# Layer 0 attention: four uneven chains of additions in place of four equal ones, row sums taken at other key tiles, five plus two buffers made four plus three

## The chip, the cores and the metric

The kernel runs on one NeuronCore of a Trainium2 chip. TensorE (PE) multiplies matrices into PSUM, ScalarE (ACT) here takes exponentials and copies PSUM out, VectorE (DVE) adds, normalizes and transposes, GpSimd (POOL) does a few powers and memsets, and SyncE issues most of the DMAs. Every engine works through its own instructions in order and waits on semaphores for the others. The metric is the device time of one execution in microseconds (us), the median of several runs. Lower is better.

## The reference

The program is a network of four layers on a tensor of 2 x 128 x 64 x 64 float32 values. The change lies in the first of the two attentions of layer 0, cut here to what matters:

```python
q1, k1, v, q2, k2 = map(to_heads, (q1, k1, v, q2, k2))      # 2 batches, 4 heads of 32 channels, 4096 tokens
q1, q2, k1, k2 = map(l2norm_tokens, (q1, q2, k1, k2))
attn1 = softmax(einsum('bhnc,bhmc->bhnm', q1, k1) * temperature, axis=-1)
out1 = einsum('bhnm,bhmc->bhnc', attn1, v)
attn2 = softmax(einsum('bhnc,bhnd->bhcd', q2, k2) * temperature, axis=-1)
out2 = einsum('bhnc,bhcd->bhnd', v, attn2)
out = out1 + out2                                            # then w_po, a norm, w_proj and the residual
```

For each query the softmax needs the sum of 4096 exponentials. Scores are bounded (the queries and keys have norm one), so the kernel takes the exponentials without a maximum, adds them up beside the product with the values, and divides at the end.

## The kernel before

**Tiling.** `attention` (from L1824) runs once for each of the two batches. The queries are cut into 8 blocks of 512 (`qb`), the keys into 32 tiles of 128 (`kt`). Its loop has 8 x 32 = 256 steps, counted by `n`; keys lie on the partitions, so a step makes a tile of weights of 128 keys x (4 heads x 512 queries), 1 MB.

**One step** has this order in the program:

1. `scores(n)` (L1850): eight matmuls into four PSUM banks. Head 0 goes to bank 6 (`single`), which every step uses again; heads 1 to 3 go to three banks (`three`) that alternate between banks 0 to 2 and 3 to 5.
2. At some steps, `totals` (L1842, operand `ones`): the row sums. Four matmuls with a matrix of ones for each of two chains of added weights, into the third bank of the other half (`banks[:, other + 2, :]`), which the step before used for scores.
3. The exponential of `single` (L1918, 512 columns) and that of `three` (L1923, 1536 columns) on ScalarE, into the tile `held[n]`, called `weights`.
4. After a `totals`, `emptied` (L1889): ScalarE copies the row sums to the tile `total`, of which there is one buffer.
5. `multiply(n - 2)` (L1842, operand `vt`): four matmuls of the weights made two steps ago with the values, gathered over the 32 key tiles in bank 7. After the last key tile ScalarE copies bank 7 to the columns of `q1` (L1863). At `kt` 1 this `multiply`, the one with the copy, stands between the two exponentials.
6. `add(n)` (L1873): VectorE adds the weights to a running sum.
7. Some steps after a `totals`, `normalized` (L1895 to L1904): VectorE turns the row sums; for the first half of a block it keeps them, for the second it adds both, takes the reciprocal, turns it back and scales the columns of `q1`.

**The chains.** `add` keeps two chains side by side, one for even and one for odd key tiles. `SUMMED = 16` restarts both every 16 key tiles, so a block of queries has four chains of 8 tiles. The first tile of a chain is not added: the chain starts as that tile of weights itself, and the second tile is added to it into a tile `sums`. No addition is thus made at `kt` 0, 1, 16 and 17, and 28 additions are made in a block. A finished chain goes to `pending`; two finished chains make a `totals`, at `kt` 18 and at `kt` 2 of the next block (`kt % SUMMED == 2`). `normalized` follows at `kt` 22 and 6.

**Side work.** At every fourth step (`n % 4 == 3`) the generator `side` is advanced: the channel attention (L1775 on), and, in the first batch, the normalization of the second batch's input, or, in the second, the statistics of the first batch's output. It puts transposes on PE, copies on ScalarE and statistics on VectorE between the steps of query blocks 0 to 5 of the first batch, and 0 to 2 of the second.

**Order.** `_in_order` ties all instructions of an engine to the order in which the program writes them, so none of them overtakes another. The pool `f0_p` holds five buffers of `weights` and two of `sums`, 1 MB each, and small tiles. A buffer is used again when all who read it are done.

Of the kernel before, what the change touches and what calls it, by code (L numbers as in the profile page):

```python
# [10 lines left out]
F32 = mybir.dt.float32  # L11
# [7 lines left out]
CH = 512  # L19
NCH = S // CH  # L20
ROWS = CH // W
NQT = S // 128
# [1262 lines left out]


LIMIT = 60.0
SUMMED = 16
F32R = mybir.dt.float32r
I32 = mybir.dt.int32  # L1290

# [157 lines left out]
def _layer0(ctx, tc, X, a, cst, worst, there, dram):  # L1449
# [8 lines left out]
    def sp():  # L1458
        n = at["pair"]
        at["pair"] = (n + 1) % 3  # L1460
        return banks[:, 2 * n : 2 * n + 2, :]

    def acc(n):
        return banks[:, 6 + n, :]

    def half():
        if at["spare"] is None:
            return sp()[:, 0, :]
        return banks[:, at["spare"].pop(0), :]
# [361 lines left out]
    def attention(pool, side):  # L1831

        sums = acc(1)
        single = banks[:, 6, :]
        parts, pending, totalled, by_query = [None, None], [], [], {}
        last = NCH * NQT - 1
        held = {}

        def four(out, lhs, w, first, stop):
            for j in range(4):  # L1840
                rows = slice(32 * j, 32 * j + 32)
                nc.tensor.matmul(out[rows, :], lhs(rows), w[:, j, :], start=first, stop=stop)  # L1842

        def scores(n, three):
            qb, kt = n // NQT, n % NQT
            for j in range(4):
                rows = slice(32 * j, 32 * j + 32)
                bank = single if j == 0 else three[:, j - 1, :]
                for h in range(2):
                    nc.tensor.matmul(  # L1850
                        bank[64 * h : 64 * h + 64, :],
                        k1[rows, kt * 128 + 64 * h : kt * 128 + 64 * h + 64],
                        q1[rows, qb * CH : (qb + 1) * CH],
                        start=True,
                        stop=True,
                    )

        def multiply(n):
            qb, kt = n // NQT, n % NQT
            w = held.pop(n)  # L1860
            four(sums, lambda rows: vt[:, kt, rows], w, kt == 0, kt == NQT - 1)
            if kt == NQT - 1:
                nc.scalar.copy(q1[:, qb * CH : (qb + 1) * CH], sums)  # L1863

        def add(n):
            p, i, w = n % 2, n % SUMMED // 2, held[n]
            if i == 0:
                parts[p] = w
            else:
                t = parts[p]  # L1870
                if i == 1:
                    parts[p] = pool.tile([128, 4, CH], F32, tag="sums", name="sums", bufs=2)
                nc.vector.tensor_add(  # L1873
                    parts[p].rearrange("p j c -> p (j c)"),
                    t.rearrange("p j c -> p (j c)"),
                    w.rearrange("p j c -> p (j c)"),
                )
            if i == SUMMED // 2 - 1:
                pending.append((n // NQT, n % NQT < SUMMED, parts[p]))

        def totals(bank):
            (qb, first, a), (_, _, b) = pending.pop(0), pending.pop(0)
            four(bank, lambda rows: ones, a, True, False)
            four(bank, lambda rows: ones, b, False, True)
            return qb, first, bank

        def emptied(qb, first, bank):
            t = pool.tile([128, CH], F32, tag="total", name="total", bufs=1)
            nc.scalar.copy(t, bank)  # L1889
            totalled.append((qb, first, t))  # L1890

        def normalized(qb, first, t):
            cols = slice(qb * CH, (qb + 1) * CH)
            turned = pool.tile([128, CH // 32, 32], F32, tag="turned", name="turned", bufs=1)
            nc.vector.transpose(turned.rearrange("p n i -> p (n i)"), t)  # L1895
            if first:
                by_query[qb] = small.tile([128, CH // 32], F32, tag="first", name="first")
                nc.vector.tensor_copy(by_query[qb], turned[:, :, 0])
                return
            rec = small.tile([128, CH // 32], F32, tag="rec", name="rec")  # L1900
            nc.vector.tensor_add(rec, turned[:, :, 0], by_query.pop(qb))
            nc.vector.reciprocal(rec, rec)
            nc.vector.transpose(turned, rec.unsqueeze(2).to_broadcast([128, CH // 32, 32]))
            nc.vector.tensor_mul(  # L1904
                q1[:, cols], q1[:, cols], turned.rearrange("p n i -> p (n i)")
            )

        for n in range(last + 1):
            kt = n % NQT
            mine, other = 3 * (n % 2), 3 * ((n + 1) % 2)  # L1910
            three = banks[:, mine : mine + 3, :]
            at["spare"] = [other, other + 1]
            held[n] = pool.tile([128, 4, CH], F32, tag="weights", name="weights", bufs=5)
            scores(n, three)
            total = None
            if len(pending) == 2 and kt % SUMMED == 2:
                total = totals(banks[:, other + 2, :])
            nc.scalar.activation(held[n][:, 0, :], single, AF.Exp)  # L1918
            if n % 4 == 3:
                next(side, None)  # L1920
            if kt == 1 and n > 1:
                multiply(n - 2)
            nc.scalar.activation(held[n][:, 1:, :], three, AF.Exp)  # L1923
            if total:
                emptied(*total)
            if kt != 1 and n > 1:
                multiply(n - 2)
            add(n)
            if totalled and kt % SUMMED == 6:
                normalized(*totalled.pop())  # L1930
        at["spare"] = None
        multiply(last - 1)
        multiply(last)
        for _ in side:
            pass
        emptied(*totals(half()))
        normalized(*totalled.pop())

# [81 lines left out]
    for b in range(B):  # L2020
        w2 = small.tile([128, 128], F32, tag="w2", name="w2")
        with tc.tile_pool(name="f0_conv", reuse_waits="tile", bufs=1) as pool, _in_order(tc):
            ss2, own = convolutions(pool, b, before)
        if b == 0:

            with _after(tc):
                rows_of_weights = _weights_by_rows(nc, dram, a)
        side = [channel_attention(ss2, own, w2)]
        if b + 1 < B:
            side.append(normalize(b + 1))  # L2030
        if b:
            side.append(
                _stats_steps(
                    nc,
                    small,
                    half,
                    X[:, b - 1, :],
                    cst,
                    mhalf,
                    there[:, b - 1],  # L2040
                    by_scalar=True,
                )
            )
        with tc.tile_pool(name="f0_p", reuse_waits="tile", bufs=4) as pool, _in_order(tc):
            attention(pool, chain(*side))
        before = finish(b, w2)
# [532 lines left out]
```

## Time and profile before

| | |
|---|---|
| median of the runs, with the lowest and the highest | 4082.22 us (4076.9 to 4084.47, 3 runs) |
| the profiled execution: its own time, and its span | 4084.82 us, 4082.9 us |
| mean granted TensorE clock | 0.98 |
| first attention, from its first exponential to its last row sum | 605.75 us (186.56 to 792.31) |
| second attention, the same | 592.07 us (980.67 to 1572.74) |
| a query block without side work | 71.75 us |
| busy share of the span: PE, DVE, ACT | 95%, 78%, 79% |
| one addition (L1873), 128 x 2048 | 2.28 us, and 2.2 us from one start to the next |

The span is the time from the first to the last instruction. In a line of a timeline the columns are the start and the duration in us, the engine, the line of the code, the operation, the tiles it writes and reads with their shapes, how many instructions are merged, and in brackets how long the engine stood idle before it and which instruction's end released it. In a line for a window they are the window, its length, the busy time of each engine with the number of its instructions, the granted clock of PE, and the DMA share and rate. PE's busy time counts matmuls that overlap each other once.

### The profile page before, as it was taken

To read this page: it belongs to the slowest core of one execution; us is meant where nothing else is said; L and a number is where in the kernel's file an instruction comes from. 1 tells how busy PE (TensorE), PEld (TensorE's weight loads), DVE (VectorE), ACT (ScalarE), POOL (GpSimd) and SP (SyncE) were. 2 spreads that over 40 slices of the span, in tenths; PEclk is the share of its full clock that TensorE was granted. 3 is DMA by queue.
4 is the path that set the end of the run, shared out by engine and by line. 5 is a ranking of instruction groups with operands and counts; after the bars stand their busy time and mean duration, and the time that the engine had idled before them with its cause. 6 is when DMAs were issued, how large, how long until landed. Compare 5 with 4: busy or idle time off the path is not lost.

```text
span 4082.9 us, 82128 instructions
## 1 busy us (share of the span) xinstructions
PE 3876.2 (95%) x35214; PEld 1325.1 (32%) x35214; DVE 3195.3 (78%) x3572; ACT 3245.5 (79%) x3955; POOL 71.1 (2%) x145
## 2 busy tenths in 40 slices
PE   7899999989999998997898999999999999999998
PEld 4511221244111113445665232232223223222222
DVE  5699898766899998986776887777777777776666
ACT  4488888735888984334654899999999999999998
POOL 1000000010000001000000000000000000000000
PEclk9999999999999999998899999999999999999999
DMA  1199970000000000003673210121012000110000
GB/s 50 23 193 187 189 95 2 1 2 2 1 2 2 2 2 13 6 1 128 256 278 112 72 35 29 36 61 32 24 32 70 27 27 29 36 54 6 6 6 4
DMA packets 193128, 217.59 MB, mean 53 GB/s; under 512 B 30441, under 2 KB 154345, under 8 KB 188658
## 3 DMA queue, kind: packets, MB, share of 16 engines
q1 hardware_dynamic: 192754, 212.25, 20.4%
q8 instruction: 278, 4.55, 0.5%
q14 instruction: 96, 0.79, 0.1%
HBM read 178.64 MB, written 98.57 MB: 68 GB/s over the span
## 4 chain that ended last, share of the span: by engine, by line
PE 63%; DVE 8%; issue 3%; ACT 1%; SPq 0%; DMA 0%; POOL 0%; DVEq 0%; POOLq 0%; ACTq 0%
PE ps_acc L2294 25%; PE ps_s L2271 18%; PE ps L1842 5%; PE ps L1850 5%; DVE X L662 3%; PE ps_bank L710 2%; PE ps_z L1008 2%; DVE e L950 1%; DVE sums L1873 1%; PE ps_bank L1062 1%; PE ps_bank L681 1%; PE ps_acc L2152 1%; PE ps_acc L2198 1%; PE ps_pe L925 1%; ACT weights L1923 1%
## 5 line engine op out<-in xcount | busy, mean ns | idle before, releaser
L2285 ACT ACTIVATE weights<-ps_s 128x1024 f32<-128x1024 f32 x1920 | 1781.5, 1062 | 76.0 <-PE ps_s L2271 75.9
L2294 PE MATMUL ps_acc<-weights,vt 128*32 128x512 f32 x8192 | 1092.9, 605 | 0.0
L1873 DVE TENSOR_TENSOR sums<-sums,weights 128x2048 f32<-128x2048 f32 x384 | 852.1, 2284 | 0.1
L2271 PE MATMUL ps_s<-q,k 64*128 64x512 f32 x4096 | 830.3, 469 | 4.2 <-DMA k<-stack 3.0
L1923 ACT ACTIVATE weights<-ps 128x1536 f32<-128x1536 f32 x512 | 741.0, 1447 | 8.5 <-PE ps L1850 8.5
L2271 PEld LDWEIGHTS ps_s<-q,k 64*128 64x128 f32 x4096 | 348.3, 184 | 936.4 <-ACT weights L2285 809.0
L1850 PE MATMUL ps<-q,k 32*64 32x512 f32 x8192 | 574.9, 613 | 3.8 <-ACT weights L1918 3.2
L1842 PE MATMUL ps<-weights,vt 128*32 128x512 f32 x4096 | 549.0, 608 | 0.0
L2243 DVE SCALAR_TENSOR_TENSOR exp_z<-exp_z,exp_m 128x1024 f32<-128x1024 f32 x384 | 469.0, 1221 | 9.3
L1918 ACT ACTIVATE weights<-ps 128x512 f32<-128x512 f32 x512 | 306.9, 599 | 88.7 <-PE ps L1850 51.5
L2227 DVE TENSOR_SCALAR exp_i<-ps_s 128x1024 int32<-128x1024 f32 x128 | 156.7, 1225 | 216.8 <-PE ps_s L2271 216.6
L2294 PEld LDWEIGHTS ps_acc<-weights,vt 128*32 128x32 f32 x8192 | 161.9, 108 | 309.4 <-issue 308.6
L1850 PEld LDWEIGHTS ps<-q,k 32*64 32x64 f32 x8192 | 120.2, 130 | 436.2 <-ACT weights L1918 381.9
L1873 DVE TENSOR_TENSOR sums<-weights 128x2048 f32<-128x2048 f32 x64 | 146.6, 2290 | 107.0 <-ACT weights L1923 97.8
L1842 PEld LDWEIGHTS ps<-weights,vt 128*32 128x32 f32 x4096 | 85.0, 108 | 395.2 <-issue 394.2
L662 DVE SCALAR_TENSOR_TENSOR X<-g,w,X 128x2048 f32<-128x2048 f32 x84 | 197.4, 2351 | 2.6
L2247 DVE SCALAR_TENSOR_TENSOR weights<-exp_z,exp_i 128x1024 f32<-128x1024 f32 x128 | 156.8, 1225 | 15.2
L2243 DVE SCALAR_TENSOR_TENSOR exp_z<-exp_m 128x1024 f32<-128x1024 f32 x128 | 155.9, 1218 | 0.0
L1008 PE MATMUL ps_z<-w_ri,e 128*32 128x128 f32 x2048 | 137.4, 409 | 14.6 <-DVE e L950 12.4
L1613 PE MATMUL ps<-pad,diag 32*32 32x512 f32 x4032 | 141.9, 603 | 4.1 <-ACT vt L1624 3.7
L1842 PE MATMUL ps<-sums,ones 128*32 128x512 f32 x512 | 70.0, 637 | 51.0 <-DVE sums L1873 32.1
L1591 PE MATMUL ps<-xn,w_qkv 128*128 128x512 f32 (+1 forms) x200 | 91.2, 605 | 19.3 <-ACT pad L1598 14.1
(304 smaller groups left out, 2995.9 us busy)
## 6 DMA issues: line engine op xcount, KB each, us to landing
w_ri<-w_r SPq DMA_DIRECT2D x16, 2112.0 KB, 8.0
w_ri<-w_i SPq DMA_DIRECT2D x16, 2112.0 KB, 13.6
stack<-qs SPq DMA_DIRECT2D x64, 256.0 KB, 2.1
q<-stack SPq DMA_DIRECT2D x128, 128.0 KB, 2.5
k<-stack SPq DMA_DIRECT2D x128, 128.0 KB, 2.6
stack<-ks SPq DMA_DIRECT2D x32, 256.0 KB, 2.1
w_r<-in_L_conv_kr_w SPq DMA_DIRECT2D x15, 528.0 KB, 12.5
w_r<-in_L_conv_kr_x SPq DMA_DIRECT2D x15, 528.0 KB, 12.4
```

Source lines behind the costliest of these rows:

```text
L662: nc.vector.scalar_tensor_tensor(xi, g[:, i : i + H // 2, j : j + W], w8[:, s : s + 1], xi, ALU.mult, ALU.add)
L1008: nc.tensor.matmul(out.rearrange("p (n f o) -> p n f o", n=2, f=2), e[:, s, 2 * j : 2 * j + 2, :].rearrange("p f x -> p (f x)"), w.rearran ...
L1842: nc.tensor.matmul(out[rows, :], lhs(rows), w[:, j, :], start=first, stop=stop)
L1850: nc.tensor.matmul(bank[64 * h : 64 * h + 64, :], k1[rows, kt * 128 + 64 * h : kt * 128 + 64 * h + 64], q1[rows, qb * CH : (qb + 1) * CH], ...
L1873: nc.vector.tensor_add(parts[p].rearrange("p j c -> p (j c)"), t.rearrange("p j c -> p (j c)"), w.rearrange("p j c -> p (j c)"),)
L1918: nc.scalar.activation(held[n][:, 0, :], single, AF.Exp)
L1923: nc.scalar.activation(held[n][:, 1:, :], three, AF.Exp)
L2243: nc.vector.scalar_tensor_tensor(z, x, n, m, ALU.add, ALU.mult)
L2247: nc.vector.scalar_tensor_tensor(w.rearrange("p j c -> p (j c)"), z, EXP_TERMS[-1], power, ALU.add, ALU.mult)
L2271: nc.tensor.matmul(ps[j // 2][:, j % 2, :], g.k[kt // 4][rows, j // 2, keys], g.q[qb][rows, j // 2, :], start=True, stop=True,)
L2285: nc.scalar.activation(w[0], ps[p], AF.Exp)
L2294: nc.tensor.matmul(g.ac[32 * j : 32 * j + 32, :], g.vt[:, kt, j // 2, i : i + 2, :].rearrange("p a d -> p (a d)"), w[:, i, :], start=(at = ...
```

## The change

`SUMMED = 16` gives way to `STARTS = (0, 1, 14, 27)`: the key tiles at which a chain starts. The even chain restarts at 14, the odd one at 27. A block of queries now has an even chain of 7 tiles (0 to 12), an odd one of 13 (1 to 25), an even one of 9 (14 to 30) and an odd one of 3 (27 to 31). No addition is made at `kt` 0, 1, 14 and 27; 28 additions are made as before.

The two `totals` of a block stand at `kt` 28 (for the chains of 7 and 13) and at `kt` 1 of the next block (for those of 9 and 3). `normalized` runs at `kt` 0 of the next block for the first and at `kt` 1 for the second; after the last block both run at the end. The exception for `kt` 1 is gone: `multiply(n - 2)` always stands behind both exponentials, and at `kt` 1 also behind `emptied`. The pool has four buffers of `weights` (its default) and three of `sums`.

```diff
 LIMIT = 60.0
-SUMMED = 16
+STARTS = (0, 1, 14, 27)
...
         def add(n):
-            p, i, w = n % 2, n % SUMMED // 2, held[n]
-            if i == 0:
+            p, kt, w = n % 2, n % NQT, held[n]
+            if kt in STARTS:
                 parts[p] = w
             else:
                 t = parts[p]
-                if i == 1:
-                    parts[p] = pool.tile([128, 4, CH], F32, tag="sums", name="sums", bufs=2)
+                if kt - 2 in STARTS:
+                    parts[p] = pool.tile([128, 4, CH], F32, tag="sums", name="sums", bufs=3)
...
-            if i == SUMMED // 2 - 1:
-                pending.append((n // NQT, n % NQT < SUMMED, parts[p]))
+            if kt + 2 in STARTS or kt + 2 >= NQT:
+                pending.append((n // NQT, kt + 2 < NQT, parts[p]))
...
-            held[n] = pool.tile([128, 4, CH], F32, tag="weights", name="weights", bufs=5)
+            held[n] = pool.tile([128, 4, CH], F32, tag="weights", name="weights")
             scores(n, three)
             total = None
-            if len(pending) == 2 and kt % SUMMED == 2:
+            if len(pending) == 2 and kt in (STARTS[-1] + 1, 1):
                 total = totals(banks[:, other + 2, :])
             nc.scalar.activation(held[n][:, 0, :], single, AF.Exp)
             if n % 4 == 3:
                 next(side, None)
-            if kt == 1 and n > 1:
-                multiply(n - 2)
             nc.scalar.activation(held[n][:, 1:, :], three, AF.Exp)
             if total:
                 emptied(*total)
-            if kt != 1 and n > 1:
+            if n > 1:
                 multiply(n - 2)
             add(n)
-            if totalled and kt % SUMMED == 6:
+            if totalled and kt < 2:
                 normalized(*totalled.pop())
         at["spare"] = None
         multiply(last - 1)
         multiply(last)
         for _ in side:
             pass
+        normalized(*totalled.pop())
         emptied(*totals(half()))
         normalized(*totalled.pop())
```

## The prediction

> **What bounds the kernel now.** I read the windows by query block first, then the timeline of one block, then the row groups. In the windows (length, then busy PE, PEld, DVE, ACT, POOL) the lines are query blocks 3 and 6 of the first attention, its sum, block 12 (the fifth of the second attention), and the second sum:
>
> ```profile
> 412.95:490.46 77.51, 73.93 (x828) 15.73 (x820) 69.94 (x65) 68.29 (x76) 5.69 (x3) 0.98 1.06 190
> 642.61:714.37 71.76, 69.06 (x804) 13.46 (x808) 64.57 (x35) 63.73 (x68) 0.00 (x0) 1.00 0.01 2
> ...
> sum 605.75, PE 575.93 PEld 119.68 DVE 545.10 ACT 524.55 POOL 16.55; mean PE 71.99 PEld 14.96 DVE 68.14 ACT 65.57 POOL 2.07
> ```
>
> ```profile
> 1279.62:1351.37 71.75, 69.06 (x804) 13.45 (x808) 65.17 (x36) 63.73 (x68) 0.00 (x0) 1.00 0.01 2
> ...
> sum 592.07, PE 564.53 PEld 112.86 DVE 530.57 ACT 510.62 POOL 3.38; mean PE 70.57 PEld 14.11 DVE 66.32 ACT 63.83 POOL 0.42
> ```
>
> PE is idle 605.75 - 575.93 = 29.8 us and 592.07 - 564.53 = 27.5 us. That is the ceiling of any gain by order alone: 57 us. In a clean block PE is idle 2.69 us. The timeline shows where:
>
> ```profile
> 1247.79 2.28 DVE L1873 TENSOR_TENSOR sums<-sums,weights 128x2048 f32<-128x2048 f32 x1
> 1248.01 1.06 PE L1842 MATMUL ps<-sums,ones 128*32 128x512 f32 x8 [0.64 <-ACT weights L1918]
> 1250.12 1.06 PE L1842 MATMUL ps<-sums,ones 128*32 128x512 f32 x8 [1.04 <-DVE sums L1873]
> ...
> 1254.02 1.11 PE L1850 MATMUL ps<-q,k 32*64 32x512 f32 x16
> 1255.06 1.06 PE L1842 MATMUL ps<-weights,vt 128*32 128x512 f32 x8
> 1256.06 1.11 PE L1850 MATMUL ps<-q,k 32*64 32x512 f32 x16
> ...
> 1282.71 0.59 ACT L1863 COPY q<-ps 128x512 f32<-128x512 f32 x1 [0.46 <-PE ps L1842]
> 1283.20 1.46 ACT L1923 ACTIVATE weights<-ps 128x1536 f32<-128x1536 f32 x1
> 1284.71 1.92 PE L1842 MATMUL ps<-sums,ones 128*32 128x512 f32 x16 [1.01 <-ACT weights L1923]
> ```
>
> A step is 1256.06 - 1254.02 = 2.04 us with no gap on PE: PE sets the pace. At `kt` 18 both chains are late: the last addition ends at 1250.07, the second half of the row sums starts at 1250.12 (the first half follows the addition before, whatever engine the bracket names). At `kt` 2 the row sums wait for the wide exponential of `kt` 1, which stood behind the copy to `q1`. Wait by wait:
>
> ```profile
> L1842 PE MATMUL ps<-sums,ones 128*32 128x512 f32 x512 | 70.0, 637 | 51.0 <-DVE sums L1873 32.1
> ```
>
> 51 of the 57 us of idle PE stand before row sums.
>
> Why is VectorE late there? I subtracted the end of each wide exponential from the start of its addition. In block 12 the lag is 0.03 us at `kt` 2, rises 0.16 to 0.17 per step (an addition every 2.20 us against a step of 2.04), jumps from 0.52 at `kt` 6 to 3.22 at `kt` 7 (the long `normalized`, 2.7 us) and is 4.58 at `kt` 15. It is 0.66 at 18, 0.03 at 19, jumps by 0.9 at 23 (the short `normalized`), and is 2.81 at 31. VectorE is slower than PE only while it adds without a break; each step without an addition gives back.
>
> [...]
>
> **The change, part by part.** Nothing is added or removed in number: 28 additions, 16 row-sum matmuls of ones in groups of four, two copies, two `normalized` a block, no DMA. S is the start of a step's scores. From the rows: the wide exponential ends at S + 3.06 (1256.06 to 1259.12), an addition can start at S + 3.09 and ends 2.29 later, at S + 5.38 + lag; row sums of a step start at S + 1.04, their second half 0.87 later.
>
> 1. *Row sums at 28.* The first half uses the chain that ended at 12. The second needs the addition at 25. Additions restart at 15 with lag 0.03 (11 steps of 0.165 to `kt` 13 make 1.85; two steps, 4.08, pass with one addition, 2.20, and give back 1.88), so the lag at 25 is 0.03 + 10 x 0.165 = 1.7. It ends at S25 + 7.1; the second half is due at S25 + 6.12 + 1.91 = S25 + 8.0. Spare 0.9: no wait. This removes 1.9 us (the first half 1247.3 to 1248.01, the second 1248.9 to 1250.12).
> 2. *Row sums at 1.* Only two steps behind the last addition, which now has lag 0.03 + 2 x 0.165 = 0.35 (three additions after the break at 27) and ends at S31 + 5.7; the second half is due at S31 + 6.0. Spare 0.3. The wide exponential of `kt` 0 ends at S31 + 5.1, the first half is due at S31 + 5.1: just met. As the copy to `q1` now stands behind both exponentials, the 1.0 us at `kt` 2 goes.
> 3. *Behind it on ScalarE at 1:* the copy of the row sums (0.59) and the copy to `q1` (0.59, 0.49 apart). Due at S + 3.1, they end at about S + 4.5; the next scores stand at S + 3.8 and need the first copy (done at S + 3.6), the next product needs the second and stands at S + 4.8. Hidden by PE's own row sums (1.74) and scores (1.04); without that cover up to 1.1 us.
> 4. *`normalized` at 0 and 1.* The long one, 2.7 us, starts after the copy, at S + 3.6, and ends at S + 6.3, where the weights of `kt` 2 come at about S + 6.9. It falls into the two steps without additions: the jump of 2.7 in the lag is gone. One new wait: the only `total` buffer is written again at 1, after VectorE has turned the sums of `kt` 28, behind the addition at 31: ready about 0.8 before it is needed.
> 5. *Four buffers of weights.* The changed program lets the narrow exponentials at 4, 5, 18 and 31 wait for the additions at 2, 3, 16 and 29, because a chain's first tile is read two steps later. The addition ends at S2 + 5.4 to 5.6; the exponential was due at S4 + 1.12 = S2 + 5.2. ScalarE is late by 0.2 to 0.4, and ends by S2 + 6.0 to 6.2, where the scores of the next step stand at S2 + 6.12. ScalarE, free after 1.83 us of a 2.04 us step, mostly hides it: 0.35 us a block, between 0 and 1.6 (four times 0.4). All other tiles have two steps more.
>
> *Clean block:* 32 x 2.04 + 2 x 1.74 (1284.71 to 1286.45) + 0.35 = 69.1, against 71.75: **-2.65**. Six such (6 and 10 to 14; 10 has a little side work): -15.9.
>
> *The two last blocks:* no next scores follow; the row sums wait for the last addition alone. Its lag falls from 2.81 to 0.35: -2.4 more each, 2 x -5.05 = -10.1.
>
> *Blocks with side work* (1 to 5, and 9): PE idle 3.6 us in block 3 (77.51 - 73.93). VectorE does 69.94 - 65.17 = 4.8 us more, in calls of about 1 us at `kt` 3, 7, 11, ... Calls at 3 to 11 lift the lag at 13 to 3 or more, so 1 to 2 us come over the break at 14, and the exponential at 18 waits; the call at 31 puts the addition at 31 1 us late, and the row sums at 1 wait about 1. An estimate from these rows: 0.3 to 1.7 at 5 and 18, 1.1 at 1, 0 to 1 at 28, about 2.5 instead of 3.6: -1.1 each, -6.6; from -2.65 to +1.
>
> *Blocks 0 and 8:* the channel attention's VectorE calls (lag at 11: 4.09) reach the exponential at 18: +1.0 each, from -1 to +3.
>
> Sum: -15.9 - 10.1 - 6.6 + 2.0 = **-30.6**. The profiled execution took 4084.8, giving 4054.2; the median is 2.6 lower, 4082.2, giving **4052**.
>
> **Rivals.**
> *A: the second row sums stay late.* VectorE is 1.7 us or more late at 31 in every block (spare 0.3 to 0.6). Then only the wait at 2 (1.0) goes, 14 blocks: about -14, 4068. For it: lags of 2 to 4 at 31 today. Against it: those come from runs of 14 additions, and this one has three.
> *B: slower, by the first tiles' buffers.* A late addition at 2, 3, 16 or 29 now stops ScalarE at once and PE 0.2 later. It decides from 2.65 / 4 = 0.7 us at each of the four places. If the long `normalized` cannot end before the weights of `kt` 2 (1.3 us later than worked), 2 and 3 are late by that, and 16 by what the break doesn't give back: 3 x 1.3 = 3.9, less 2.65, times 16: +20, 4102. For it: side blocks. Against: the lag at 2 is 0.03 in all 16 blocks.
> *C: every wait goes,* in side blocks too: -57 + about 5, 4030. Against it: VectorE is 90% busy there.
> *D: the gain is given back* by something outside the two attentions: no change. The DMA that runs beside the first one ends by 642 of 792 us, so nothing in flight waits.
>
> **How the numbers follow.** Main 0.72, A 0.12, B 0.09, C 0.04, D 0.03. Main alone reaches from 4037 (six side blocks like clean ones, -9.3, and no 0.35 in 16 blocks, -5.6) to 4069 (side blocks unchanged, +6.6, and 1.6 instead of 0.35 in the eight other blocks, +10). The range takes these ends and A in: 4036 to 4070. Faster by over 0.2% (8 us, about what a measurement of this kernel tells from no change): main, A, C: 0.88; same 0.03; slower 0.09.
>
> **What would show it.** Clean blocks at 69.1 with PE idle 0.2 to 0.5; no idle before row sums at 28; lag at 31 near 0.35 and at 7 near 0.85; narrow exponentials at 4, 5, 18 and 31 released by DVE `sums`. I am wrong if clean blocks stay above 70.5, if `normalized` at 1 pushes the addition at 2, or if side blocks grow.

## The result, and the profile after

| | before | after |
|---|---|---|
| median, lowest and highest (6 runs each) | 4081.84 us (4076.9 to 4084.47) | 4051.27 us (4046.65 to 4055.79) |
| ratio, with its 95% interval | | 0.9925 [0.9914, 0.9936] |
| profiled execution: own time, span | 4084.82, 4082.9 us | 4055.79, 4054.0 us |
| first attention, first exponential to last row sum | 605.75 us | 593.79 us |
| second attention | 592.07 us | 571.80 us |

The change makes the kernel 0.75% faster. The two attentions give 32.2 us; outside them the profiled execution is 3.3 us longer, of which 1.9 lie before the first attention starts. That start wanders from 180.4 to 188.5 us between the profiles of this case, so these 3.3 us are not laid to the change.

The windows by query block, after, for the first attention (blocks 0, 3, 6 and the sum; columns: length, then busy PE, PEld, DVE, ACT, POOL, then the granted clock):

```profile
188.50:270.02 81.52, 75.77 (x818) 17.48 (x820) 65.69 (x48) 63.70 (x73) 0.86 (x2) 0.96 1.15 180
...
414.97:489.32 74.35, 72.52 (x824) 15.53 (x820) 70.33 (x65) 68.18 (x77) 5.69 (x3) 1.00 1.03 186
...
639.43:708.69 69.26, 69.05 (x804) 13.54 (x804) 65.37 (x36) 63.51 (x69) 0.00 (x0) 1.00 0.01 2
...
sum 593.79, PE 576.85 PEld 120.83 DVE 547.20 ACT 523.10 POOL 23.27; mean PE 72.11 PEld 15.10 DVE 68.40 ACT 65.39 POOL 2.91
```

The same for the second attention, block 12 and the sum:

```profile
1259.95:1329.21 69.26, 69.05 (x804) 13.54 (x804) 65.37 (x36) 63.51 (x69) 0.00 (x0) 1.00 0.01 2
...
sum 571.80, PE 561.64 PEld 113.36 DVE 531.89 ACT 508.93 POOL 16.60; mean PE 70.21 PEld 14.17 DVE 66.49 ACT 63.62 POOL 2.07
```

PE is now idle 593.79 - 576.85 = 16.9 us and 10.2 us, from 29.8 and 27.5. A clean block takes 69.26 us with 0.21 us of idle PE. But block 0 grew from 76.82 to 81.52, at a clock of 0.96 where it had been 1.00.

The timeline where block 12 begins, after:

```profile
1258.12 0.60 ACT L1918 ACTIVATE weights<-ps 128x512 f32<-128x512 f32 x1 [0.38 <-DVE sums L1873]
...
1261.95 1.92 PE L1842 MATMUL ps<-sums,ones 128*32 128x512 f32 x16
...
1263.94 0.59 ACT L1889 COPY total<-ps 128x512 f32<-128x512 f32 x1
1264.56 0.71 DVE L1895 STREAM_TRANSPOSE turned<-total 128x512 f32<-128x512 f32 x1 [1.29 <-ACT total L1889]
...
1264.80 0.59 ACT L1863 COPY q<-ps 128x512 f32<-128x512 f32 x1 [0.27 <-PE ps L1842]
...
1267.81 4.49 DVE L1873 TENSOR_TENSOR sums<-weights 128x2048 f32<-128x2048 f32 x2 [0.50 <-ACT weights L1921]
...
1270.20 0.60 ACT L1918 ACTIVATE weights<-ps 128x512 f32<-128x512 f32 x1 [0.38 <-DVE sums L1873]
```

The row sums at `kt` 1 (1261.95) have no bracket: PE goes straight into all eight matmuls. The long `normalized` begins at 1264.56, and VectorE then stands idle 0.50 us before the addition at `kt` 2. The brackets on the narrow exponentials are the new wait for a buffer: 0.38 us, which costs PE next to nothing here.

The row groups, after (busy, mean ns, then the engine's idle time before the group, by releaser):

```profile
L1850 PE MATMUL ps<-q,k 32*64 32x512 f32 x8192 | 577.0, 615 | 21.6 <-ACT weights L1918 19.4
...
L1918 ACT ACTIVATE weights<-ps 128x512 f32<-128x512 f32 x512 | 306.8, 599 | 107.1 <-DVE sums L1873 38.6
...
L1842 PE MATMUL ps<-sums,ones 128*32 128x512 f32 x512 | 64.0, 599 | 1.6 <-DVE sums L1873 0.6 <-ACT weights L1921 0.4
```

The group of the scores before:

```profile
L1850 PE MATMUL ps<-q,k 32*64 32x512 f32 x8192 | 574.9, 613 | 3.8 <-ACT weights L1918 3.2
```

Idle PE before row sums fell from 51.0 us to 1.6. Idle PE before scores rose from 3.8 to 21.6: a part of the old wait came back as a wait for narrow exponentials, which wait for VectorE. The costliest places are at `kt` 18 of blocks 0 and 8; the timeline of block 0, after:

```profile
237.25 6.69 DVE L1873 TENSOR_TENSOR sums<-sums,weights 128x2048 f32<-128x2048 f32 x3
237.43 0.60 ACT L1918 ACTIVATE weights<-ps 128x512 f32<-128x512 f32 x1 [2.66 <-DVE sums L1873]
...
238.08 1.12 PE L1850 MATMUL ps<-q,k 32*64 32x512 f32 x16 [2.49 <-ACT weights L1918]
...
239.85 1.94 PE L1842 MATMUL ps<-weights,vt 128*32 128x512 f32 x8
...
241.71 1.59 PE L1850 MATMUL ps<-q,k 32*64 32x512 f32 x16
```

ScalarE stops 2.66 us for the addition at `kt` 16, PE 2.49 us behind it. Then `multiply` takes 1.94 us where it takes 1.06 elsewhere: the granted clock is 0.50 from 239.33 to 242.75 us, and 1.00 again behind it. Such a stretch is called halved clock below.

### The profile page after: what moved, and what is told of

Its sections match the earlier page's. It is cut to its first block, busy times and chain, and to the rows that moved or that the text cites. A ratio compares the mean times of both kernels' runs of the same rounds, so it can differ in the third digit from the quotient of the medians.

```text
span 4054.0 us, 82178 instructions
## 1 busy us (share of the span) xinstructions
PE 3872.8 (96%) x35214; PEld 1324.0 (33%) x35214; DVE 3198.9 (79%) x3572; ACT 3242.3 (80%) x3955; POOL 90.7 (2%) x145
## 3 DMA queue, kind: packets, MB, share of 16 engines
q1 hardware_dynamic: 192754, 212.25, 20.3%
## 4 chain that ended last, share of the span: by engine, by line
PE 65%; DVE 7%; ACT 2%; issue 2%; POOL 0%; SPq 0%; DMA 0%; ACTq 0%; POOLq 0%; DVEq 0%
PE ps_acc L2293 25%; PE ps_s L2270 18%; PE ps L1842 5%; PE ps L1850 5%; PE ps_bank L710 2%; DVE sums L1873 2%; PE ps_z L1008 2%; DVE e L950 2%; PE ps_t L640 1%; PE ps_bank L590 1%; PE ps_bank L681 1%; PE ps_bank L1062 1%; PE ps_acc L2151 1%; PE ps_acc L2197 1%; PE ps_pe L925 1%
## 5 line engine op out<-in xcount | busy, mean ns | idle before, releaser
L1873 DVE TENSOR_TENSOR sums<-sums,weights 128x2048 f32<-128x2048 f32 x384 | 855.3, 2287 | 15.8 <-ACT weights L1921 14.5
L1850 PE MATMUL ps<-q,k 32*64 32x512 f32 x8192 | 577.0, 615 | 21.6 <-ACT weights L1918 19.4
L1918 ACT ACTIVATE weights<-ps 128x512 f32<-128x512 f32 x512 | 306.8, 599 | 107.1 <-DVE sums L1873 38.6
L1873 DVE TENSOR_TENSOR sums<-weights 128x2048 f32<-128x2048 f32 x64 | 145.9, 2289 | 39.8 <-ACT weights L1921 39.3
L2246 DVE SCALAR_TENSOR_TENSOR weights<-exp_z,exp_i 128x1024 f32<-128x1024 f32 x128 | 156.8, 1225 | 15.9 <-ACT weights L2284 0.5
L950 DVE TENSOR_SCALAR e<-ps_pe 32x136 f32<-32x136 f32 (+1 forms) x352 | 104.3, 296 | 4.9
```

The costliest lines, as they stand in the source:

```text
L950: nc.vector.tensor_scalar_mul(out, got[of, :, s], sign)
L1850: nc.tensor.matmul(bank[64 * h : 64 * h + 64, :], k1[rows, kt * 128 + 64 * h : kt * 128 + 64 * h + 64], q1[rows, qb * CH : (qb + 1) * CH], ...
L1873: nc.vector.tensor_add(parts[p].rearrange("p j c -> p (j c)"), t.rearrange("p j c -> p (j c)"), w.rearrange("p j c -> p (j c)"),)
```

## The experiments

My theory was the prediction's: VectorE's lag reaches places where PE waits, and the change keeps it from there. The rival accounts give the credit to other parts: to the uneven chains, to the place of `normalized`, to the late copy, or to the later row sums. No kernel here leaves out work. Kernels 1 to 4 ran on one chip, 5 to 8 on another, 9 and 10 on a third, each against the kernel before on the same chip.

### 1. The late copy alone

The kernel before, with the `multiply` and copy of `kt` 1 behind both exponentials:

```diff
-            if kt == 1 and n > 1:
-                multiply(n - 2)
             nc.scalar.activation(held[n][:, 1:, :], three, AF.Exp)
...
-            if kt != 1 and n > 1:
+            if n > 1:
```

> The kernel before with one edit: the product with the copy to q1 stands behind both exponentials at kt 1 too. Theory (three separate losses in a block: 1.0 us at kt 2 by the copy, 1.9 us at kt 18 by late additions, 0.2 to 0.5 us by first tiles where there are only four buffers): the 1.0 us in front of the row sums at kt 2 goes, but the second half of them then meets the addition at 31 (lag 2.81, spare 2.65), so about 0.8 us a block is left of it: clean blocks 70.9 instead of 71.75, the whole 9 to 15 us faster. Rival (the copy only changes place: the product of kt 0 waits for it instead): clean blocks 71.75, no change.

Measured: 4067.75 us, ratio 0.9966 [0.9951, 0.998], 13.3 us faster; a clean block takes 70.86. Row group:

```profile
L1842 PE MATMUL ps<-sums,ones 128*32 128x512 f32 x512 | 70.3, 625 | 39.3 <-DVE sums L1873 35.2 <-ACT weights L1918 3.8
```

The wait for the wide exponential at `kt` 2 is gone; what is left is released by VectorE. As the theory had it.

### 2. The place of `normalized` alone

The kernel before, its chains even, with `normalized` at `kt` 16 and 0, the steps without additions:

```diff
-            if totalled and kt % SUMMED == 6:
+            if totalled and kt % SUMMED == 0:
                 normalized(*totalled.pop())
...
+        normalized(*totalled.pop())
         emptied(*totals(half()))
```

> The kernel before with one edit: normalized at kt 16 and 0, where no addition is made, in place of kt 22 and 6. Chains, row sums, buffers and the copy are as before. Theory: the lag at kt 15 falls from 4.6 to about 2.2, the row sums at kt 18 don't wait, those at 2 still wait 1.0 for the exponential: clean blocks 69.7, the whole about 30 us faster, as much as the whole change. Rival (the uneven chains and the row sums at 28 and 1 bring the gain, and normalized could have stayed): under 10 us.

Measured: 4041.48 us, ratio 0.99 [0.9884, 0.9917], 39.6 us faster, more than the whole change and more than the 30 expected; a clean block takes 69.83.

```profile
L1842 PE MATMUL ps<-sums,ones 128*32 128x512 f32 x512 | 63.6, 606 | 23.3 <-ACT weights L1923 14.2 <-DVE sums L1873 9.1
```

Here VectorE's share falls from 32.1 to 9.1 us, and the wide exponential behind the copy stays: 14.2 us, 1.0 in 14 blocks. So the break in the additions was there before; it was only not used for `normalized`.

### 3. Both, with even chains

The two edits above together.

> The two edits together: equal chains of 8, five and two buffers, row sums at 18 and 2, normalized at 16 and 0, the copy behind both exponentials. Theory: both waits go, and as no first tile's buffer is short, clean blocks are 68.7 to 69.3, and the blocks with side work, whose additions are late by 1 to 2 us at first tiles in the changed kernel, gain more than there: 36 to 42 us faster than the kernel before, 6 to 12 faster than the changed one. Rival (the uneven chains are needed for the row sums not to meet the last addition): clean blocks 70 or more, slower than the changed kernel.

Measured: 4030.66 us, ratio 0.9874 [0.9858, 0.9891], 50.4 us faster, more than the 36 to 42 expected. It beats both kernels.

```profile
L1842 PE MATMUL ps<-sums,ones 128*32 128x512 f32 x512 | 64.2, 605 | 11.4 <-DVE sums L1873 11.4
```

The window of its block 6:

```profile
620.57:689.39 68.82, 68.82 (x804) 13.54 (x808) 64.81 (x36) 63.51 (x67) 0.00 (x0) 1.00 0.01 2
```

The idle times add up: 51.0 less 11.7 (experiment 1) less 27.7 (experiment 2) is 11.6, and 11.4 was measured. A clean block has no idle PE at all. The rest stands in blocks with side work and in the last ones. The uneven chains are not needed for the gain.

### 4. The changed kernel with five buffers

The changed kernel with five buffers of `weights` beside three of `sums`. To make room, `total` and `turned` lie in parts of other tiles that are unused by then:

```diff
-            held[n] = pool.tile([128, 4, CH], F32, tag="weights", name="weights")
+            held[n] = pool.tile([128, 4, CH], F32, tag="weights", name="weights", bufs=5)
...
-            t = pool.tile([128, CH], F32, tag="total", name="total", bufs=1)
+            t = spare("total")
...
-            turned = pool.tile([128, CH // 32, 32], F32, tag="turned", name="turned", bufs=1)
+            turned = spare("turned").rearrange("p (n i) -> p n i", i=32)
```

> The changed kernel with five buffers of weights beside three of sums. The pool has no room for that, so the small tiles total and turned lie in columns of xn that nobody reads then, late in the first batch in the two y buffers. Theory (first tiles' buffers cost 0.2 to 0.5 us in clean blocks and 2.5 us in blocks 0 and 8): no narrow exponential is released by DVE sums any more at kt 4, 5, 18 and 31, clean blocks 68.7 instead of 69.25, blocks 0 and 8 about 2 us shorter, the whole 8 to 12 us faster than the changed kernel. Rival (ScalarE's slack hides these waits, the loss in the side blocks is VectorE's own time): within 3 us of the changed kernel.

Measured: 4032.05 us, ratio 0.9882 [0.9866, 0.9899], 49 us faster than before and so some 18 faster than the changed kernel, more than the 8 to 12 expected. The profiles have 20.3 us between the attentions of the two, of which four stretches of halved clock (the last table) make 6.1. Its two row groups (the same lines stand six or seven further down in its code):

```profile
L1856 PE MATMUL ps<-q,k 32*64 32x512 f32 x8192 | 574.5, 612 | 6.3 <-ACT weights L1925 5.6
L1848 PE MATMUL ps<-sums,ones 128*32 128x512 f32 x512 | 64.5, 600 | 6.9 <-DVE sums L1879 5.9 <-ACT weights L1928 0.4
```

The idle time before scores falls from 21.6 to 6.3: it was the doing of having four buffers only, for the waits of narrow exponentials for VectorE fall from 38.6 to 5.8 us, and in clean blocks to none. (That `total` and `turned` moved is no rival: in the changed kernel the copy to `total` waits for PE alone, 6.5 us in all.) Blocks 0 and 8 shrink from 81.52 and 79.86 to 75.73 and 75.74; of that, three stretches of halved clock make 4.6 by the same count. With enough buffers, uneven chains (4032.05) and even ones (4030.66) can't be told apart.

### 5. The uneven chains without the better place of `normalized`

The changed kernel with `normalized` at `kt` 6 and 7, where additions run:

```diff
-            t = pool.tile([128, CH], F32, tag="total", name="total", bufs=1)
+            t = pool.tile([128, CH], F32, tag="total", name="total", bufs=2)
...
-            if totalled and kt < 2:
-                normalized(*totalled.pop())
+            if totalled and kt in (6, 7):
+                normalized(*totalled.pop(0))
```

> The changed kernel with normalized at kt 6 and 7 instead of 0 and 1 (and two buffers of total, which this needs). Uneven chains, row sums at 28 and 1, the late copy and four and three buffers stay. Theory (VectorE's lag at the places where somebody waits for it is all that counts, and normalized is what raised it): both fall into the chain of 13, the lag at 13 is 0.03 + 1.85 + 3.6 = 5.5, 3.6 come over the break at 14, the addition at 16 is that late and the narrow exponential at 18 waits for its buffer: clean blocks about 72.4, longer than before the change, the whole 0 to 15 us slower than the kernel before. Rival (uneven chains and new places of the row sums bring most of the gain): 15 us or more faster than the kernel before.

Measured: 4103.05 us, ratio 1.0059 [1.0042, 1.0076], 25 us slower than before. The direction was expected, the size was not (0 to 15 was). Its row groups:

```profile
L1850 PE MATMUL ps<-q,k 32*64 32x512 f32 x8192 | 582.5, 619 | 60.5 <-ACT weights L1918 54.2
...
L1842 PE MATMUL ps<-sums,ones 128*32 128x512 f32 x512 | 64.0, 599 | 1.6 <-DVE sums L1873 0.6 <-ACT weights L1921 0.4
```

No row sums wait, yet it is the slowest kernel of all: 60.5 us of waiting stand before scores instead. The timeline of block 12 at `kt` 18:

```profile
1334.91 6.69 DVE L1873 TENSOR_TENSOR sums<-sums,weights 128x2048 f32<-128x2048 f32 x3
1335.09 0.60 ACT L1918 ACTIVATE weights<-ps 128x512 f32<-128x512 f32 x1 [2.66 <-DVE sums L1873]
...
1335.74 1.14 PE L1850 MATMUL ps<-q,k 32*64 32x512 f32 x16 [2.48 <-ACT weights L1918]
```

The lag is 1.44 us at `kt` 7 and 4.26 at 8, 4.49 at 13, and 2.48 at 15 to 17: the break at 14 gives back 2 us. The first tile of the chain that starts at 14 is read at 16, and with four buffers the exponential at 18 needs it. This is the prediction's rival B, a late addition at 16 stopping ScalarE and PE, by another road. The windows of blocks 11 and 12 show what made it larger:

```profile
1220.13:1292.67 72.54, 69.43 (x804) 13.54 (x804) 65.27 (x36) 63.49 (x69) 0.00 (x0) 1.00 0.01 1
1292.67:1366.77 74.10, 71.00 (x804) 13.71 (x803) 65.35 (x36) 63.50 (x69) 0.00 (x0) 0.98 0.01 2
```

The same wait costs 1.56 us more in block 12 than in 11, and PE's busy time grows by that: the clock was halved once. Blocks 13 and 14 repeat the pair.

### 6. Later row sums alone

The kernel before, with its row sums at `kt` 20 and 4:

```diff
-            if len(pending) == 2 and kt % SUMMED == 2:
+            if len(pending) == 2 and kt % SUMMED == 4:
```

> The kernel before with the row sums two steps later, at kt 20 and 4, and nothing else changed. Theory: VectorE stays as late as it is (lag 4.6 at 15), but the row sums come 4.08 us later, so the spare is 6.7 instead of 2.65 and PE does not wait at them: clean blocks 69.4 to 70.0, the whole 24 to 32 us faster, as the changed kernel. The first additions of the next chains must wait for their buffer of sums until then, and are late by about 3 us at 18, which nobody notices. Rival (VectorE's lateness costs PE elsewhere, through buffers of weights, when the row sums don't meet it): clean blocks above 71.

Measured: 4047.56 us, ratio 0.9924 [0.9907, 0.994], 30.4 us faster; a clean block takes 69.61. Both are as expected.

```profile
L1850 PE MATMUL ps<-q,k 32*64 32x512 f32 x8192 | 575.5, 613 | 13.4 <-ACT weights L1918 11.3
L1842 PE MATMUL ps<-sums,ones 128*32 128x512 f32 x512 | 64.1, 616 | 9.6 <-DVE sums L1873 6.8 <-ACT weights L1923 2.5
```

The lag was expected to stay at 4.6 us at `kt` 15 and rises to 6.25, because the first additions of the chains now wait for their buffer of `sums` (lag 3.08 at `kt` 2). PE hardly meets it: in a clean block it is idle 0.68 us. Only the last row sums of each attention wait for it, 3.3 and 3.5 us, and the last blocks stay long (79.4 and 78.6 us, from 77.9). Here lag cost only where it exceeded the spare time of the one who waited. So later row sums alone, with `normalized` where it was, bring as much as the whole change.

### 7. The changed kernel with the early copy

```diff
+            if kt == 1 and n > 1:
+                multiply(n - 2)
             nc.scalar.activation(held[n][:, 1:, :], three, AF.Exp)
...
-            if n > 1:
+            if kt != 1 and n > 1:
```

> The changed kernel with the product and the copy at kt 1 between the two exponentials again. Theory: there the row sums now stand in the same step, so the product, the copy behind it and the wide exponential of kt 1 come about 1.7 us later, and with them the copy of the row sums whose bank the next scores need: clean blocks 71.2 to 71.8, and most of the gain goes: 0 to 6 us faster than the kernel before. Rival (ScalarE's slack hides the copy wherever it stands): clean blocks 69.3, as the changed kernel.

Measured: 4092.93 us, ratio 1.0037 [1.0025, 1.005], 15 us slower than before. A clean block at 71.65 was as expected; the time was not.

```profile
L1850 PE MATMUL ps<-q,k 32*64 32x512 f32 x8192 | 594.2, 618 | 38.2 <-ACT total L1889 21.1 <-ACT weights L1918 15.5
```

With row sums at `kt` 1, the early copy stands behind PE's row sums and holds back the wide exponential, the copy of the row sums and so the next scores: a clean block is 2.4 us longer than the changed kernel's 69.26, and 1.5 of them are idle PE before scores at `kt` 2. The late copy is thus a condition of the changed kernel's row sums at 1. The profiled execution took 4082.66 us, the other runs about 4092 to 4095, so ten microseconds of the miss differ from run to run of one kernel.

### 8. Even chains with four plus three buffers

Kernel 3 with the buffers of the changed kernel:

```diff
-                    parts[p] = pool.tile([128, 4, CH], F32, tag="sums", name="sums", bufs=2)
+                    parts[p] = pool.tile([128, 4, CH], F32, tag="sums", name="sums", bufs=3)
...
-            held[n] = pool.tile([128, 4, CH], F32, tag="weights", name="weights", bufs=5)
+            held[n] = pool.tile([128, 4, CH], F32, tag="weights", name="weights", bufs=4)
```

> The third experiment (equal chains, normalized at 16 and 0, late copy) with four buffers of weights and three of sums in place of five and two. Theory (a fourth buffer instead of a fifth costs only where an addition two steps behind a first tile is late, and here the additions at 2 and 3 follow a break, those at 18 and 19 are late by about 1 us, in steps in which PE's row sums give ScalarE 1.74 us more): within 5 us of the third experiment, clean blocks 68.7 to 69.3. Rival (four buffers cost 19 us whatever the chains, as between the changed kernel and the fourth experiment): 4050.

Measured: 4033.39 us, ratio 0.9889 [0.9873, 0.9906], 44.6 us faster; a clean block takes 68.92. The median is 2.7 us above kernel 3's, the gain on its own chip 5.8 smaller, and the attentions 2.0 longer; the intervals of the two overlap. So four buffers cost even chains little, where they cost uneven ones some 18 us. The even chains leave two neighbouring steps without additions (4.08 us at `kt` 16 and 17) before a chain's first tile is read, where the uneven ones leave one at 14. That this is the reason is argued from the lags, not shown.

### 9. Kernel 7 again, on a third chip

> The seventh experiment once more on another chip, since its profiled execution took 4082.7 and its other runs 4092 to 4095. If the profile tells the whole of it (clean blocks 71.65, both attentions together as long as before the change), the runs are within 0.1% of the kernel before. If something outside the profile costs 10 us with this kernel, they are again 0.3% slower, and what that is stays open.

Measured over 14 runs: 4092.76 us (4079.93 to 4102.69), ratio 1.0027 [1.0014, 1.004]. The windows of blocks 11, 12 and 14, which do the same work:

```profile
1211.21:1284.40 73.19, 71.57 (x804) 13.83 (x804) 65.45 (x36) 63.52 (x68) 0.00 (x0) 0.98 0.01 2
1284.40:1359.12 74.72, 73.10 (x804) 13.98 (x804) 65.54 (x36) 63.50 (x68) 0.00 (x0) 0.95 0.01 1
...
1432.36:1504.02 71.66, 70.04 (x804) 13.70 (x804) 65.36 (x36) 63.42 (x69) 0.00 (x0) 1.00 0.01 1
```

PE's timeline in the second of them:

```profile
1291.71 1.51 PE L1850 MATMUL ps<-q,k 32*64 32x512 f32 x4 [1.51 <-ACT total L1889]
1293.15 1.94 PE L1842 MATMUL ps<-weights,vt 128*32 128x512 f32 x8
1295.02 2.01 PE L1850 MATMUL ps<-q,k 32*64 32x512 f32 x16
1296.96 1.94 PE L1842 MATMUL ps<-weights,vt 128*32 128x512 f32 x8
```

71.66, 73.19 and 74.72 are steps of 1.53 us: none, one and two stretches of 3.4 us at half clock. After a gap of 1.51 us, `multiply` takes 1.94 us instead of 1.06.

The runs are again 0.3% slower, but not by something outside the profile: this profile, of a run of 4097.14 us, has twelve such stretches within the attentions, that of experiment 7, of a run of 4082.66, six. The mean granted clock of a run goes with its time: here from 0.980 at 4079.93 us to 0.975 at 4102.69, in experiment 7 from 0.980 in the profiled run to 0.977 or 0.978 in the five others. By an estimate from these figures, 0.005 of the span is 20 us of lost clock, twelve stretches, 18 of the 22.8 us between the fastest run and the slowest.

### 10. Kernel 3 with the side work one step later

```diff
-            if n % 4 == 3:
+            if n % 4 == 0:
                 next(side, None)
```

> The third experiment with the side work advanced at n % 4 == 0 instead of 3. Theory (what is left of idle PE in blocks 0 and 8 comes from the channel attention's VectorE calls in the chain before kt 18, and PE's wait of 1.3 us for the first of them at kt 3): blocks 0 and 8 are 1.0 to 1.5 us shorter, clean blocks stay at 68.8, the other blocks move by less than 1 us: 2 to 4 us faster than the third experiment. Rival (the place of the calls doesn't matter as their work is the same): blocks 0 and 8 as long as in the third experiment.

Measured: 4035.83 us, ratio 0.9893 [0.9876, 0.9909]. Blocks 0 and 8 take 77.46 and 77.43 us, in kernel 3 78.76 and 76.83; the attentions 1148.4 against 1148.5. The expected gain is not there in the time. But block 8 has a stretch of halved clock here that it doesn't have in kernel 3, and block 0 has one in both: without them both blocks are shorter, by 1.3 and 0.9 us, about as expected.

### The kernels side by side

All from the profiled executions. Idle PE before row sums and before scores are the two row groups; the attentions are the sum of both, against 1197.8 us before; halved clock is the time within them at a clock of 0.5. The last column is an estimate: it takes 1.53 us for each 3.4 us of halved clock out of the difference, on both sides (before: 20.5 us, six stretches).

| kernel | before row sums | before scores | attentions | halved clock | without it |
|---|---|---|---|---|---|
| before | 51.0 | 3.8 | | 20.5 | |
| changed | 1.6 | 21.6 | -32.2 | 13.7 | -29.2 |
| 1 late copy | 39.3 | 3.8 | -14.9 | 10.2 | -10.3 |
| 2 `normalized` | 23.3 | 3.9 | -38.4 | 3.4 | -30.8 |
| 3 both | 11.4 | 3.9 | -49.3 | 3.4 | -41.6 |
| 4 five buffers | 6.9 | 6.3 | -52.5 | 0 | -43.3 |
| 5 late `normalized` | 1.6 | 60.5 | +18.9 | 30.7 | +14.3 |
| 6 later row sums | 9.6 | 13.4 | -31.4 | 12.3 | -27.7 |
| 7 early copy | 1.6 | 38.2 | +1.3 | 20.5 | +1.3 |
| 8 even, four plus three | 8.6 | 6.8 | -47.3 | 3.4 | -39.7 |
| 9 early copy again | 1.6 | 39.8 | +12.0 | 40.9 | +2.8 |
| 10 side work later | 10.6 | 2.9 | -49.4 | 6.8 | -43.3 |

Without the halved clock, experiments 1 and 2 add up to experiment 3 (-10.3 - 30.8 = -41.1 against -41.6), and experiment 2 alone is worth the whole change. The forecasts of experiments 2, 3 and 5, which the measured times miss by some 8 to 10 us, fit the last column.

## Why the prediction was right, point by point

The total held: -30.6 us on the profiled execution was forecast, -29.0 measured (4084.82 to 4055.79), and 4052 against a median of 4051.27. That it came so close is in part luck, as its terms show. By these, the halved clock counted at 1.53 us a stretch:

| term | forecast | measured | of it halved clock | rest |
|---|---|---|---|---|
| six clean blocks (6, 10 to 14) | -15.9 | -14.4 | 0 | -14.4 |
| two last blocks (7, 15) | -10.1 | -9.4 | 0 | -9.4 |
| six side blocks (1 to 5, 9) | -6.6 | -14.5 | -6.1 | -8.4 |
| blocks 0 and 8 | +2.0 | +6.1 | +3.1 | +3.0 |
| sum, from unrounded lengths | -30.6 | -32.2 | -3.1 | -29.2 |

The stretches went in blocks 1, 3 (one each) and 9 (two), and came in block 0 (two); blocks 5 and 8 have one in both profiles.

- **An addition's price and PE's order** are as the terms took them. The median addition into a running sum takes 2.284 us before and 2.287 after, the first of a chain 2.292 in both. PE keeps the program's order: before, the product at 1251.01 starts behind the late row sums at 1250.12, though its weights had been complete since 1245.25.
- **Parts 1 and 2** (row sums at 28 and 1) held. Idle PE before all row sums is 1.6 us. The lag in block 12 is 1.48 us at `kt` 25 (forecast 1.7), 0.61 at 7 (0.85) and 0.09 at 31 (0.35): a little lower, as an exponential that waits for a buffer comes later itself. With five buffers (experiment 4) the three lags are 1.82, 0.85 and 0.36.
- **Part 3** (copies hidden) held: 0.21 us of idle PE in a clean block, with `emptied` and the copy 0.27 us apart. Experiment 7 shows what the order is worth.
- **Part 4** (`normalized`) held: 0.50 us are left before the addition at `kt` 2. The one buffer of `total` is no wait; it is turned at 1262.35 to 1263.05 and written at 1263.94, with 0.9 to spare where 0.8 was forecast.
- **Part 5** (four buffers) was right in clean blocks (0.21 us of idle against 0.35) and named the right places elsewhere: 16.3 of the 21.6 us of idle PE before scores follow the exponentials at `kt` 18 and 5. In blocks 0 and 8 they are 2.49 and 2.76 us at 18.
- **The mis-sized terms** are the side blocks (-1.1 forecast, -2.4 measured in the mean) and blocks 0 and 8 (+1.0, and +4.7 and +1.35 measured). Their errors, 7.9 us of gain and 4.1 of loss, half cancelled, and the 3.3 us outside the attentions, which no term foresaw, took the total back nearer to the forecast: that is the luck. Without the halved clock they are -1.4 a side block and +1.6 and +1.35: the waits were sized about right, and most of what the sum lacked was a term for the clock. The profile before showed it: the clock of 0.98 in its own window of block 3, which I had quoted and not used.
- **The smaller misses:** clean blocks 10 and 11 gained 2.2, not 2.65.

The rivals: A fell (lag 0.09 at 31, and 1.5 us of wait at 1 in all sixteen blocks), C and D did not come about. B didn't decide here, but the stop that it describes is real: experiment 5 has it, at +25 us, of which halved clock is some 5.

What the prediction could not tell is which part earns the gain. It priced the removed waits under the row sums' new places and gave `normalized`, its part 4, no price of its own. The runs turn that round: `normalized` in the steps without additions is worth 39.6 us by itself with even chains, the late copy 13.3, both 50.4; the uneven chains with `normalized` among the additions lose 25. With the same buffers and the late copy, and `normalized` in steps without additions, even chains gain 44.6 (experiment 8) and the changed kernel 30.6: its uneven chains, with the places of their row sums, cost 14 us there. Five buffers take that loss away (experiment 4). The gains don't add throughout, as several edits go round one wait: later row sums alone give 30.4, and need no other part.

Open: why one execution of a kernel has more halved clock than another. The profile of experiment 9 is 14.5 us longer than that of 7, 10.7 of it within the attentions; its six stretches more explain 9. On the chip of experiment 7, runs with the same granted clock of 0.980 take 4082.66 us with its kernel and 4086.3 with the kernel before. By these figures its 15 us are for the most part not longer waits, but waits followed more often by halved clock.

## What to carry to other kernels

When an engine with some slack holds up the bound one, write down its lag step by step and look for the jump, then move the job that makes the jump into steps where that engine has nothing else to do, before changing the shape of the work: that move alone gave 39.6 us in experiment 2. Count who reads the oldest buffer and how late that reader runs: here one buffer fewer turned harmless lag into a stop of the engine that fills it (idle PE before scores 6.3 us with five buffers, 21.6 with four). A wait taken away in one row group may stand in another, as when the row sums' fell from 51.0 to 1.6 us and the scores' rose from 3.8 to 21.6, so compare the idle columns of all groups of the bound engine.

## What the runs showed of the hardware

A gap of 1.5 to 2.5 us on PE can be followed by half clock. In block 12 of experiment 9 a gap of 1.51 us stands before two stretches of 3.4 us, and the block takes 74.72 us where one without them takes 71.66; in block 12 of experiment 5 a gap of 2.48 us stands before one, 74.10 against 72.54. That is 1.53 and 1.56 us a stretch. Within the attentions the records have a clock of 0.5 or 1.0 only. The 44 stretches at 0.5 that begin there, in twelve profiles, are 3.41 or 6.83 us long and begin, in each profile, on one grid of 3.413 us. With the changed kernel they begin at 201.79, 239.33, 580.67 and 1017.57 us: the last three come 11, 111 and 239 times 3.4133 us behind the first.

For each cell of that grid one can count how long PE was busy, by its matmul records, whose ends are modelled. Of the cells at full clock, all 25 with PE busy for less than 44% were followed by half clock, none of the 3972 with 64% or more, and 19 of the 60 between. In the profiles before and after the change alone it is all 8, none of 662, and 1 of 9. So in these profiles the same gap has a price or none, by where it falls: the gap of 2.48 us of experiment 5 lies within one cell in block 12 (PE busy 28%) and is parted between two in block 11 (busy 71% and 53%). A gap of less than half a cell was enough: 1.51 us in one cell, busy 56%, in block 12 of experiment 9. Part of what a removed wait returns is the clock: by the estimate of the last table about 8 of 49 us in experiment 3. No edit moved a gap against the grid on purpose, so that its place decides rests on this count; what sets the clock is not shown.
